# Cross-attention block on one core: the two key halves of the value product moved into the innermost loop

## The chip, the core and the metric

The kernel runs on one core of a Trainium2 chip. The metric is the device time of one execution in microseconds (us). Three executions of the kernel before took 1031.25 us (median), from 1029.74 to 1033.43.

The engines are named as the profile names them: PE is the matrix engine, PEld its loading of weights, DVE the vector engine, ACT the scalar engine, POOL the general engine, SP the engine that issues most transfers. PE writes its results to PSUM, which this kernel uses as eight banks of 512 floats on each of 128 partitions. A matmul of 32 contraction rows and 32 result columns stands in the profile as `32*32`. The kernel places such matmuls by the partitions of the operands (`32c`, the tile's row) and of the result (`32r`, its column); with four of each these are sixteen places, called tiles here.

## The reference

Sixteen batches, 1024 queries and 64 keys each, width 512, 16 heads of 32. Cut to what matters here:

```python
xq  = _ada_ln(x_q,  t_vec, Wss_q,  bss_q)      # layer norm, scale and shift from the condition
xkv = _ada_ln(x_kv, t_vec, Wss_kv, bss_kv)
q   = (xq @ Wq + bq).reshape(B, Lq, nh, dh)
kv  = (xkv @ Wkv + bkv).reshape(B, Lkv, 2, nh, dh)
k, v = kv[:, :, 0], kv[:, :, 1]
scores = jnp.einsum('bqhd,bkhd->bhqk', q, k) / jnp.sqrt(jnp.float32(dh))
attn = jax.nn.softmax(scores, axis=-1)
out  = jnp.einsum('bhqk,bkhd->bqhd', attn, v).reshape(B, Lq, H)
return x_q + (out @ Wp + bp)
```

The change is in the product of `attn` and `v`. Everything is float32.

## The kernel before

The queries are cut into 32 blocks of 512 (`TB`), two to a batch; `i` counts the blocks. The order of all work is written out by hand: after a prologue for the keys, the values and blocks 0 to 2, a loop from line 1404 on runs over blocks 3 to 29, and the last blocks are written out again. In one turn `i` of the loop PE does, in this order and with other products between them: the scores of block `i` (`scores`), the value product of block `i-1` (`mix(a)`), the output projection of blocks `i-2` and `i-1` (`product`), and the query projection of block `i+1` (`query_product`). The two projections use seven products of half blocks in place of eight.

The 64 keys of a batch are two halves of 32, counted by `z`. The scores and the weights of a block lie in two tiles, `s_tiles[i, 0]` and `s_tiles[i, 1]`, one for each half: partitions `32c` to `32c+31` hold the 32 keys of the half for head group `c` (`NC` = 4 groups), and `r` counts the four heads of a group (`HPC` = 4). DVE takes maxima (`maximum`), POOL subtracts them (`subtract`), ACT exponentiates (`weights`), and POOL adds the two halves (`total`) for the row sums, whose inverse comes back through DRAM (`inverse_rows`, `spread_rows`).

`mix(i)` makes the value product. For half `z`, group `c` and head `r` one matmul takes the 32x32 values `vt[rows, z, 32r:32r+32]` as weights and the 32x512 weights of the queries `p[rows, r, :]` as the moving operand, and writes partitions `32r` to `32r+31` of bank `po[c]`. Its array tile is thus row `c`, column `r`: sixteen tiles, each used once for each half, 32 matmuls in all. The second half adds to what the first has written. The loops before are `z` outermost, then `c`, then `r`: a tile is used again after the fifteen others. In 31 of the 32 blocks the four banks are two pairs from the pool that the scores use too (`ps_s`); in block 29 (`apart=False`) they are four single banks.

`divided(i)` on DVE multiplies the finished banks by the inverse row sums and writes `ot`, one pair of banks after the other; `row_sums` on POOL and `product` on PE read `ot`.

The row of the trace for a matmul carries the line of the call: L826 is the matmul of `mix`, L658 that of the scores, L539 that of the query projection (and of the keys' and values'), L955 that of the output projection, L853 and L871 those of its plain form in the first and last blocks. Every float32 matmul that is no transpose is four rows in the trace: a weight load and a product, and then a second weight load and a second product on the same tile.

Of the kernel before, what the change touches and what calls it, by code (L numbers as in the profile page):

```python
# [20 lines left out]
def cross_attention_block(  # L21
# [24 lines left out]
    NC = H // P  # L46
    HPC = P // DH
# [31 lines left out]
    def bank(name, k=None):  # L79
        if k is None:  # L80
            k = ring.pop(0)
            ring.append(k)
        return ps_m.tile([P, TB], F32, tag=f"mm{k}", name=name)
# [563 lines left out]
    s_tiles, m_tiles = {}, {}  # L647
# [162 lines left out]
    def mix(i, apart=True, ks=(None,) * NC):  # L810

        vt = v_tiles[i // BPB]

        if apart:
            pairs = [ps_s.tile([P, 2, TB], F32, tag="s", name=f"po_{i}_{e}") for e in range(2)]
            po = [pairs[c // 2][:, c % 2, :] for c in range(NC)]
            po_tiles[i] = pairs
        else:
            po = [bank(f"po_{i}_{c}", ks[c]) for c in range(NC)]
            po_tiles[i] = po  # L820
        for z in range(2):
            p = s_tiles.pop((i, z))
            for c in range(NC):
                rows = slice(32 * c, 32 * c + 32)
                for r in range(HPC):
                    nc.tensor.matmul(  # L826
                        po[c][32 * r : 32 * r + 32, :],
                        lhsT=vt[rows, z, 32 * r : 32 * r + 32],
                        rhs=p[rows, r, :],
                        start=(z == 0),  # L830
                        stop=(z == 1),
                    )
# [443 lines left out]
    query_out(2, 2)  # L1276
    hidden(4, (0,))
    mix(0)
    subtract(1, zs=(0,))
    spread_rows(0)  # L1280
# [67 lines left out]
    hidden(5, (1,))  # L1348
    query_product(3, 6)
    mix(1)  # L1350
    copied(2, 1, 1)
    copied(2, 1, 0)
# [51 lines left out]
    for i in range(3, NB - 2):  # L1404
# [24 lines left out]
        biased(a, 2)  # L1429
        load_residual(i)  # L1430
        mix(a)
        divided(a)
        row_sums(a, 0)
# [44 lines left out]
    y, z = NB - 2, NB - 1  # L1478
# [134 lines left out]
```

## Time and profile before

| what | before |
|---|---|
| time, median of 3 runs | 1031.25 us (1029.74 to 1033.43) |
| span of the profiled execution | 1029.1 us |
| PE busy | 1009.3 us (98%) |
| weight loads (PEld) busy | 763.4 us (74%) |
| DVE busy | 860.9 us (84%) |
| POOL busy | 805.9 us (78%) |
| ACT busy | 638.6 us (62%) |
| granted TensorE clock, mean | 0.998 |

The profiled execution is one run of the program under the profiler; its span goes from its first to its last instruction, 1029.1 us, and lies 2.1 us under the median of the timed runs. Busy time counts an engine as busy as long as at least one of its rows lasts. The ends of PE's rows are modelled from the size of the instruction, so rows of PE overlap, and what a product costs is read from the starts of successive rows. The chain of waits follows the work back from the last instruction and says at each step what released it. A column `x64` counts rows; a view cut to a stretch of time counts the rows that overlap it. Idle time of an engine that is not the bottleneck costs nothing.

### The profile page before, as it was taken

Reading aid. Unit: us, or ns where it says so; the run is one execution under the profiler, and the core shown is the slowest. Engines: PE = TensorE matmul, PEld = TensorE weight load, DVE = VectorE, ACT = ScalarE, POOL = GpSimd, SP = SyncE. Lnnn points to the kernel's source line nnn. Section 1 sums busy time; section 2 is a strip of 40 time slices with the busy share of each in tenths; the row PEclk is TensorE's granted clock in tenths of the full one; section 3 lists DMA queues with packets and bytes.
Section 4 is the critical chain, followed back from the end, with each engine's and each line's share of the span. In section 5 each row is a group of like instructions: output and inputs, shape, how many; then the busy total and the mean of one; then the engine's idle time right before and its main releaser. Section 6 shows DMA issues by size and latency. Waiting matters only on the chain.

```text
span 1029.1 us, 21212 instructions
## 1 busy us (share of the span) xinstructions
PE 1009.3 (98%) x8077; PEld 763.4 (74%) x8077; DVE 860.9 (84%) x1174; ACT 638.6 (62%) x1025; POOL 805.9 (78%) x518
## 2 busy tenths in 40 slices
PE   8999899999999999999999999999999999999998
PEld 7877556777777777777777778777777777777746
DVE  6686669889888888889898888898888888876795
ACT  3786565666666666667666666666666676665530
POOL 4566687798888888898888888988888888987861
PEclk9999999999999999999999999999999999999999
DMA  9563544444544444445444444445434444335122
GB/s 318 179 188 119 149 122 136 157 157 156 165 155 121 143 128 154 152 152 166 140 134 146 150 133 153 156 159 165 148 110 151 134 154 154 113 125 166 46 85 85
DMA packets 112197, 149.82 MB, mean 146 GB/s; under 512 B 34104, under 2 KB 45392, under 8 KB 112096
## 3 DMA queue, kind: packets, MB, share of 16 engines
q1 hardware_dynamic: 111712, 147.94, 45.3%
q8 instruction: 64, 1.05, 0.4%
q0 software_dynamic: 384, 0.54, 0.3%
q14 instruction: 37, 0.30, 0.1%
HBM read 79.21 MB, written 34.60 MB: 111 GB/s over the span
## 4 chain that ended last, share of the span: by engine, by line
PE 81%; SPq 6%; DMA 5%; DVE 4%; ACT 1%; issue 1%; POOL 1%; DVEq 0%; ACTq 0%; POOLq 0%
PE pp L955 34%; PE pq L539 33%; PE po L826 6%; PE ps L658 6%; SPq L387 4%; DMA ltd<-lt 1%; SPq L631 1%; PE pk_A L539 1%; PE pv_A L539 1%; DMA xt<-ht 1%; DMA r<-in_x_dram 1%; DVE ht L365 1%; DVE lt L762 1%; DMA wss_kv<-in_L_xcond_Wss_kv_dram 1%; DMA x<-in_x_dram 1%
## 5 line engine op out<-in xcount | busy, mean ns | idle before, releaser
L717 POOL TENSOR_TENSOR s<-s,mb 128x2048 f32<-128x2048 f32 x64 | 290.2, 4558 | 129.3 <-DVE mb L704 127.7
L684 ACT COPY s<-ps 128x1024 f32<-128x1024 f32 x128 | 129.4, 1012 | 108.1 <-DVE m L675 64.8
L675 DVE TRANSPOSE_TENSOR_REDUCE m<-ps 128x32 f32<-128x1024 f32 x128 | 150.7, 1213 | 33.6 <-PE ps L658 33.4
L955 PE MATMUL pp<-w_p_sb,ot 128*128 128x256 f32 x720 | 165.6, 379 | 0.5 <-DVE r L979 0.4
L979 DVE TENSOR_TENSOR r<-pp,r 128x512 f32<-128x512 f32 x203 | 131.8, 670 | 30.9 <-PE pp L955 24.3
L578 ACT ACTIVATE qt<-pq,bias_t 128x256 f32<-128x256 f32 x256 | 105.6, 463 | 77.2 <-PE pq L539 77.0
L955 PEld LDWEIGHTS pp<-w_p_sb,ot 128*128 128x128 f32 x720 | 136.6, 190 | 20.5 <-issue 1.6
L723 ACT ACTIVATE s<-s 128x2048 f32<-128x2048 f32 x64 | 122.3, 1911 | 43.8 <-POOL s L717 43.8
L757 POOL TENSOR_TENSOR sum<-s,s 128x2048 f32<-128x2048 f32 x31 | 140.7, 4540 | 7.0 <-ACT s L723 7.0
L955 PEld LDWEIGHTS pp<-WT,s 128*128 128x128 f32 x480 | 86.5, 189 | 57.0 <-issue 37.7
L539 PE MATMUL pq<-xt_sums,w_q_sums 128*128 128x256 f32 x512 | 123.3, 385 | 0.0
L539 PE MATMUL pq<-xt,w_q_sums 128*128 128x256 f32 x512 | 121.1, 379 | 1.6 <-DVE qt L585 1.6
L539 PE MATMUL pq<-xt,w_q_sb 128*128 128x256 f32 x512 | 121.6, 380 | 0.3 <-ACT pq L551 0.2
L539 PEld LDWEIGHTS pq<-xt_sums,w_q_sums 128*128 128x128 f32 x512 | 94.9, 190 | 36.5 <-issue 24.8
L955 PE MATMUL pp<-WT,s 128*128 128x256 f32 x480 | 119.3, 391 | 0.2 <-POOL s L934 0.2
L955 PE MATMUL pp<-WT,ot 128*128 128x256 f32 x480 | 113.6, 379 | 0.6 <-POOL ot L931 0.6
L539 PEld LDWEIGHTS pq<-xt,w_q_sb 128*128 128x128 f32 x512 | 96.8, 190 | 16.4 <-issue 1.7
L539 PEld LDWEIGHTS pq<-xt,w_q_sums 128*128 128x128 f32 x512 | 97.2, 190 | 15.2 <-DVE qt L585 2.0
L955 PEld LDWEIGHTS pp<-WT,ot 128*128 128x128 f32 x480 | 91.0, 190 | 14.1 <-POOL ot L931 1.0
L335 ACT ACTIVATE x<-x,rstdq 128x512 f32<-128x512 f32 x128 | 97.0, 807 | 4.4 <-POOL rstdq L312 4.4
L447 ACT ACTIVATE xt<-xt,ss_q 128x512 f32<-128x512 f32 x124 | 93.9, 808 | 5.1 <-DMA xt<-ht 4.5
L498 POOL TENSOR_TENSOR xt_sums<-xt 128x512 f32<-128x512 f32 x64 | 81.4, 1272 | 14.2 <-ACT xt L447 7.3
(176 smaller groups left out, 1509.8 us busy)
## 6 DMA issues: line engine op xcount, KB each, us to landing
x<-in_x_dram SPq DMA_DIRECT2D x32, 1024.0 KB, 5.5
r<-in_x_dram SPq DMA_DIRECT2D x32, 1024.0 KB, 5.1
xt<-ht SPq DMA_DIRECT2D x488, 64.0 KB, 2.0
out_dram<-r SPq DMA_DIRECT2D x58, 512.0 KB, 3.7
out_dram<-r SPq DMA_DIRECT2D x11, 256.0 KB, 2.2
wss_kv<-in_L_xcond_Wss_kv_dram SPq DMA_DIRECT2D x4, 512.0 KB, 7.3
wss_q<-in_L_xcond_Wss_q_dram SPq DMA_DIRECT2D x4, 512.0 KB, 11.0
vr<-ltd SPq DMA_DIRECT2D x128, 8.0 KB, 1.6
```

Source lines behind the costliest of these rows:

```text
L335: nc.scalar.activation(dst, src, AF.Identity, bias=rstd[:, 1, j : j + 1], scale=rstd[:, 0, j : j + 1])
L447: nc.scalar.activation(xt[:, :, c, :], xt[:, :, c, :], AF.Identity, scale=ss["q"][:, c, b : b + 1], bias=ss["q"][:, NC + c, b : b + 1],)
L498: eng.tensor_tensor(dst, a, b, ALU.subtract)
L539: nc.tensor.matmul(out_, lhsT=lhsT, rhs=rhs, start=new and m == 0 and c == 0, stop=c == HC - 1, skip_group_check=True,)
L578: nc.scalar.activation(dst, src, AF.Identity, bias=bq_t[:, o : o + 1])
L675: nc.vector.tensor_reduce(m_tiles[i][:, z, 2 * e : 2 * e + 2, :], s_banks[i, z][e].rearrange("p r (j a) -> p r j a", a=32), AX.X, ALU.max, ...
L684: nc.scalar.copy(s_tiles[i, z][:, 2 * e : 2 * e + 2, :], s_banks[i, z][e])
L717: eng.tensor_tensor(s_tiles[i, z], s_tiles[i, z], mb_tiles[i], ALU.subtract)
L723: nc.scalar.activation(p, p, AF.Exp, scale=SCALE)
L757: nc.gpsimd.tensor_tensor(t, s_tiles[i, 0], s_tiles[i, 1], ALU.add)
L955: nc.tensor.matmul(acc[k][:, t * HO : (t + 1) * HO], lhsT=rows[:, c, t * P : (t + 1) * P], rhs=cols[:, c, :], start=n == 2 and t == 0 and ...
L979: nc.vector.tensor_add(r, a, r)
```

## The change

In `mix`, both tiles of weights are taken out of `s_tiles` ahead of the loops, and the loop over the halves becomes the innermost one:

```diff
-        for z in range(2):
-            p = s_tiles.pop((i, z))
-            for c in range(NC):
-                rows = slice(32 * c, 32 * c + 32)
-                for r in range(HPC):
+        p = [s_tiles.pop((i, z)) for z in range(2)]
+        for c in range(NC):
+            rows = slice(32 * c, 32 * c + 32)
+            for r in range(HPC):
+                for z in range(2):
                     nc.tensor.matmul(
                         po[c][32 * r : 32 * r + 32, :],
                         lhsT=vt[rows, z, 32 * r : 32 * r + 32],
-                        rhs=p[rows, r, :],
+                        rhs=p[z][rows, r, :],
                         start=(z == 0),
                         stop=(z == 1),
                     )
```

The 32 matmuls of a block, their operands, their tiles and their banks are the same. Their order on PE is now tile by tile, the two halves of a tile directly behind each other. No other instruction of any engine is added, removed or moved against the others.

## The prediction, on record before the changed kernel had run

> **What bounds the kernel now.** I read the page first, then the chain of waits, then windows from one value product to the next.
>
> ```profile
> PE 1009.3 (98%) x8077; PEld 763.4 (74%) x8077; DVE 860.9 (84%) x1174; ACT 638.6 (62%) x1025; POOL 805.9 (78%) x518
> PE 81%; SPq 6%; DMA 5%; DVE 4%; ACT 1%; issue 1%; POOL 1%; DVEq 0%; ACTq 0%; POOLq 0%
> ...
> 206.64:235.83 29.19, 29.19 (x242) 22.31 (x241) 25.88 (x35) 19.16 (x30) 24.41 (x16) 1.00 0.48 150
> 907.27:936.46 29.19, 29.19 (x242) 22.31 (x241) 22.74 (x27) 15.49 (x21) 23.63 (x12) 1.00 0.36 112
> ```
>
> The last two rows are stretches from the start of one value product to the next (length, then PE, PEld, DVE, ACT, POOL busy, granted clock). PE is busy for all of 29.19 us, the next engine for 25.88. There are (936.46 - 206.64) / 29.19 = 25 such turns, so 26 value products stand where each nanosecond that PE loses is lost by the kernel. The other six stand ahead of 206.64 (three) or behind 936.46 (three), where others wait too.
>
> So the question is how long PE needs for 32 matmuls on sixteen tiles in the new order. One value product in the middle of the run, matmuls and weight loads, in rows of ever narrower windows:
>
> ```profile
> L826 PE MATMUL po<-s,V_A x1024: 584/588/612, 107.0 to 558.7; 32*32 32x512 f32 x171
> ...
> 527.76 0.23 PEld L826 LDWEIGHTS po<-s,V_A 32*32 32x32 f32 x32 [0.33 <-ACT x L335]
> 528.22 0.10 PEld L826 LDWEIGHTS po<-s,V_A 32*32 32x32 f32 x1 [0.22 <-issue]
> 528.65 0.10 PEld L826 LDWEIGHTS po<-s,V_A 32*32 32x32 f32 x1 [0.33 <-issue]
> 528.84 0.12 PEld L826 LDWEIGHTS po<-s,V_A 32*32 32x32 f32 x2
> 528.65 0.55 PEld L826 LDWEIGHTS po<-s,V_A 32*32 32x32 f32 x31 [0.33 <-issue]
> 529.53 0.59 PE L826 MATMUL po<-s,V_A 32*32 32x512 f32 x1
> 530.04 0.48 PE L539 MATMUL pq<-xt_sums,w_q_sums 128*128 128x256 f32 x1
> ...
> 527.87:528.21 0.34, 0.34 (x16) 0.13 (x31) 1.00 0.27 66
> 528.23:528.33 0.10, 0.10 (x32) 0.10 (x1) 1.00 0.37 82
> 528.66:528.83 0.17, 0.17 (x17) 0.10 (x1) 1.00 0.05 12
> ```
>
> The 1024 rows on V_A belong to 16 blocks of 32 matmuls, so a matmul is two products (a pass each) and two weight loads. What the rows show, from the start at 527.77:
>
> - All 32 loads of the first half are issued within 0.23 us, and until 528.21 exactly sixteen products are in flight: the first pass of every tile. The program's order is first and second pass of tile 0, then tile 1; so products of different tiles do overtake each other, and a tile does its own in order.
> - Tile 0's passes follow its weight loads' release: second pass at 528.22 (0.45 us after the first), first pass of the other key half at 528.65 (0.43 later). Four passes of one tile in a row thus start over 0.45 + 0.43 + 0.43 = 1.31 us.
> - Between 528.66 and 528.83 there are 17 products: 16 old ones and tile 0's third. Tiles 1 to 15, free from 528.66 on, get nothing: the next load comes at 528.84. Something holds back the 35th load.
> - From there the remaining 30 loads (31 rows from 528.65, without that one) are spread up to 529.20 less 0.10 for the last, 529.10: 0.26 us for 15 tiles, 0.017 us for the four instructions of a matmul. In the first half they came at 0.10 / 15 = 0.007 (32 loads in 0.23, of which 0.10 is the last one's length and 0.03 its lag behind the first).
> - The product of another shape starts 0.51 us behind the last start (529.53 to 530.04). Total: 2.28 us.
>
> What holds the 35th load? Sixteen matmuls are 64 instructions, and the loads fit a **queue of 64** places that come free in program order, each when its instruction is over by its modelled end. Load 33, a product and load 34 are instructions 65 to 67 and get the places of tile 0's first three; instruction 68 needs the place of the fourth, tile 0's second pass, which ends at 528.22 + 0.588 = 528.81, and load 35 is right behind it: 0.03 us later. The first value product of the run, which had only eight products under way where the other has sixteen, tells this from a drain of the whole array:
>
> ```profile
> 107.06:107.09 0.03, 0.03 (x8) 0.03 (x17) 1.00 0.24 68
> 527.85:527.88 0.03, 0.03 (x16) 0.03 (x29) 1.00 1.89 410
> ...
> 107.43 0.10 PEld L826 LDWEIGHTS po<-s,V_A 32*32 32x32 f32 x1
> ...
> 108.05 0.10 PEld L826 LDWEIGHTS po<-s,V_A 32*32 32x32 f32 x1
> ```
>
> These are its 33rd load (at tile 0's second pass) and its 35th: 107.43 + 0.588 + 0.03 = 108.05, the same distance, although its later tiles were late. The Trainium skill says in "TensorE: Matmul & The Clock Gate", section "Architectural detail: the array is 16× 32×32, not 1× 128×128", that TensorE's queue is 64 deep and a partial reorder window; the trace agrees with its 64 places.
>
> **The change part by part.** It removes and adds no instruction; it reorders 32 matmuls in each of 32 blocks (2 x 1024 rows, 64 to a block). Now a tile has eight instructions one behind the other, so 64 places hold eight tiles, not sixteen. Step by step, from the start of a block:
>
> 1. Tiles 0 to 7 enter at 2 x 0.007 us from each other and do their four passes side by side: starts at 0, 0.45, 0.88, 1.31, the last pass over at 1.31 + 0.59 = 1.90.
> 2. Tile 8's instructions take the places of tile 0's as these end: its first pass at 0.61 + 0.03 = 0.64, its last at 1.93.
> 3. Tile 9 needs the places of tile 1, which come free only behind all of tile 0's: 1.90 + 0.03 = 1.93. Tiles 9 to 15 then enter at 2 x 0.017 us from each other; tile 15 starts at about 2.14.
> 4. Tile 15's last pass starts at 2.14 + 1.31 = 3.45, and the next product 0.51 behind it: 3.96 us.
>
> So a block needs 3.96 us for 2.28, **1.68 us more**; the pause of 0.19 us at 528.65 and the slower entry are gone, and a wait of half the tiles for the other half has come.
>
> Does anything cover it? Within a turn no: PE has no idle time. What is queued behind on PE all moves with it. On DVE, `divided` takes the first pair of banks about when it did (tile 7's last pass is over at 1.99; before, the pair was taken at 2.3), the second pair at about 4.1 (3.45 + 0.59):
>
> ```profile
> 530.08 2.36 DVE L806 TENSOR_TENSOR ot<-po,vb 128x1024 f32<-128x1024 f32 x2 [0.43 <-issue]
> 532.04 3.45 PE pp L955 x16
> ```
>
> With half of 2.36 us for a pair it is done at 5.3, 1.3 us behind the end of the value product on PE; `product` with the first pair starts 1.92 behind that (530.12 to 532.04) and with the second 1.73 later, so no new wait. DVE's 25.88 us of work have room in 30.87.
>
> The six at the ends. PE waits there for others, and the lost time goes into those waits:
>
> ```profile
> PE pp L871 <- ACT pp L866: 2.9, 1, 2.9
> PE pq L539 <- DVE qt L585: 1.6, 1, 1.6
> PE pq L539 <- ACT qt L578: 1.3, 1, 1.3
> ...
> 116.36 10.26 DMA r<-in_x_dram
> 152.75 2.06 DMA xt<-ht
> 181.02 0.39 DMA xt<-ht
> ...
> 188.40 3.69 PE pq L539 x16
> ```
>
> The chain of waits runs through the residual's load at 116.36 and the moves at 152.75 and 181.02, not through PE; PE takes it over at 188.40. Block 0's 1.68 goes into the wait of 2.9, block 1's into the 1.6, block 2's into the 1.3, with 0.35 left over. At the end:
>
> ```profile
> 979.75 0.70 PE L853 MATMUL pp<-w_p_sb,ot 128*128 128x512 f32 x1 [0.68 <-DVE ot L801]
> 983.01 1.19 DVE L675 TRANSPOSE_TENSOR_REDUCE m<-ps 128x32 f32<-128x1024 f32 x1
> ...
> 992.53 3.70 PE L853 MATMUL pp<-w_p_sb,ot 128*128 128x512 f32 x8
> 997.35 0.65 DVE L882 TENSOR_TENSOR r<-pp,r 128x512 f32<-128x512 f32 x1
> ...
> 1010.31 1.99 PE L955 MATMUL pp<-WT,ot 128*128 128x256 f32 x8
> 1012.44 3.72 PE L955 MATMUL pp<-w_p_sb,ot 128*128 128x256 f32 x16
> 1016.36 1.59 PEld L955 LDWEIGHTS pp<-WT,s 128*128 128x128 f32 x8 [0.60 <-POOL s L934]
> ```
>
> Block 29: the scores behind it are wanted by DVE only at 983.01, so nothing. Block 30: L853 ends at 996.23 + 1.68 = 997.91, and DVE, which took it at 997.35, takes it at about 997.95: 0.6. Block 31: the eight rows at 1010.31 go to 1011.99, 1.73 for them and 3.45 for the sixteen (3.45 for sixteen rows at 532.04) bring PE to 1017.18, where it waited until 1016.36: 0.8.
>
> Sum: 26 x 1.68 = 43.7, and 0.35 + 0.6 + 0.8: **45.4 us**. The profiled execution goes from 1029.1 to 1074.5; the median of the runs lies 2.15 above that span, so 1031.25 + 45.4 = **1076.6 us**.
>
> The bounds. The trace shows no tile with more than four instructions waiting or under way, so what PE does with eight on one tile is not shown. From below: were no place short, a block would be 1.31 + 15 x 0.013 + 0.51 = 2.02 us, 0.26 less than now. From above: were tile 1 held until tile 0 has taken its fourth load (0.88), 15 x 0.88 + 1.31 + 0.51 = 15.0 us, 12.8 more. I take the queue of 64, since it gives the 2.28 and the pause of the old order from the same rows.
>
> **The rivals.**
>
> *A tile takes only its next weights, and the queue stops there.* Tile 0's instructions for the other half wait for its first half, and tile 1's stand behind them: 12.8 us a block. 32 x 12.8 = 410, less the 2.9 + 1.6 + 1.3 of waits ahead and 3 x 1.68 - 1.4 = 3.6 behind: about 1430 us. For it: weights 33 and 34 came only when tile 0 took them (528.22, 528.65). Against it: tiles did pass a waiting pass of tile 0, and the 35th load waited for 528.81, not 528.65. 0.11. A stricter form: products start in the program's order. A tile would have to start its fourth pass before the next starts its first: 16 x 1.31 + 0.51 = 21.5 us, 19.2 more a block, some 1640 us. Sixteen first passes under way before any second speak against it. 0.01. (The Trainium skill has this as a rule, "TensorE: Matmul & The Clock Gate", section "The mechanism": matmuls start and end in strict order. The trace disagrees.)
>
> *Faster: the pause was the price of coming back to a tile late, not of a full queue.* Then tile 8 finds place at once, and each of 26 blocks, and part of the six, gains 0.26: 7 to 8 us, 1024 us. It decides if tile 9's first pass starts within 0.2 us of tile 0's. For it: the pause stands just where tiles are used again. Against it: it ended with tile 0's pass, in both blocks. 0.05.
>
> *No change that can be measured.* Between the two, with something like 0.1 us a block. 0.03. That the order is not what the change says can be left out: PE's order is written by hand.
>
> **How the numbers follow.** 0.80 for the forecast, 0.11, 0.01, 0.05, 0.03. This kernel's measurement can tell 0.3% from no change (3 us). Slower 0.92, same 0.03, faster 0.05. Within the forecast: all 32 blocks paid in full give 32 x 1.68 = 53.8, 1085 us; a tile's entry at 0.017 for all and a queue a few places off move a block by 0.2, some 6 us either way. 1062 to 1092 holds the forecast's case, and with it 8 in 10.
>
> **What would show it.** In the changed kernel a stretch between value products of 30.87 us with PE busy throughout; in the value product sixteen weight loads of eight tiles in the first 0.2 us, one tile more at 0.6, seven from 1.93 on; the last start near 3.45. It is wrong if tile 9 starts before 1.8 us or tile 1 after 0.1, or if PE shows new waits for DVE L806.

## The result: 4.4% slower, and the profile after

The changed kernel takes 1077.11 us (median of 4 runs, 1076.26 to 1078.6) against 1031.62 us for the kernel before (4 runs): a ratio of 1.044, 95% interval 1.0423 to 1.0457. The prediction was 1076.6 us. The profiled execution spans 1076.8 us, 47.7 more than before; the other three runs span 1074.5 to 1075.4.

The page of the changed kernel, engines first, then the chain of waits by engine and by line:

```profile
PE 1061.0 (99%) x8077; PEld 798.0 (74%) x8077; DVE 866.6 (80%) x1174; ACT 641.4 (60%) x1025; POOL 805.3 (75%) x518
PE 89%; DMA 4%; SPq 3%; DVE 2%; ACT 1%; POOL 1%; issue 1%; DVEq 0%; POOLq 0%
PE pp L955 34%; PE pq L539 33%; PE po L826 11%; PE ps L658 6%; SPq L387 2%; PE pp L853 1%; PE pk_A L539 1%; PE pv_A L539 1%; DMA r<-in_x_dram 1%; DMA xt<-ht 1%; DMA ltd<-lt 1%; DMA wss_kv<-in_L_xcond_Wss_kv_dram 1%; POOL sum L757 0%; POOL s L717 0%; DVE ht L365 0%
```

The counts are those of before, PE's busy time is up by 51.7 us, and the value product (L826) has gone from 6% of the chain to 11%. The other engines do the same work in a longer span, so their shares fall.

Stretches from the start of one value product to the next, changed kernel:

```profile
207.84:238.71 30.87, 30.87 (x241) 23.35 (x240) 26.08 (x35) 19.27 (x30) 24.36 (x16) 1.00 0.47 140
948.70:979.57 30.87, 30.87 (x241) 23.35 (x240) 22.97 (x27) 15.60 (x21) 23.61 (x12) 1.00 0.36 108
```

A turn is 30.87 us for 29.19, PE busy for all of it, at a granted clock of 1.00: 1.68 us a turn.

One value product of the changed kernel (it starts at 609.14), weight loads of the whole block, then single loads, the last product and the first of another shape, then how many products and loads are in flight in four stretches:

```profile
609.14 0.23 PEld L826 LDWEIGHTS po<-s,V_B 32*32 32x32 f32 x17 [0.33 <-ACT x L335]
609.60 0.72 PEld L826 LDWEIGHTS po<-s,V_B 32*32 32x32 f32 x18 [0.23 <-issue]
610.64 0.10 PEld L826 LDWEIGHTS po<-s,V_B 32*32 32x32 f32 x1 [0.33 <-issue]
611.07 1.19 PEld L826 LDWEIGHTS po<-s,V_B 32*32 32x32 f32 x28 [0.33 <-issue]
612.59 0.59 PE L826 MATMUL po<-s,V_B 32*32 32x512 f32 x1
613.11 0.48 PE L539 MATMUL pq<-xt_sums,w_q_sums 128*128 128x256 f32 x1
...
609.25:609.59 0.34, 0.34 (x8) 0.12 (x16) 1.00 0.11 30
609.70:609.78 0.08, 0.08 (x16) 0.08 (x8) 1.00 0.85 230
611.00:611.07 0.07, 0.07 (x9) 0.00 (x0) 1.00 0.70 176
611.30:611.50 0.20, 0.20 (x8) 0.11 (x7) 1.00 0.01 0
```

Read it against the block of before. There, 32 loads went out at once and sixteen tiles worked; here it is 17 loads (two for each of tiles 0 to 7, and tile 8's first), and until 609.59 exactly eight products are in flight: tiles 0 to 7. They take their second passes from 609.60 on; the sixteen products at 609.70 are the first and second passes of these same eight tiles, because the first ones are still in flight by their modelled ends. Tile 8 takes tile 0's places one by one, the fourth load at 610.64. Tile 9 gets its first load at 611.07, when tile 0's last pass is over (609.14 + 1.90 = 611.04), and the 28 loads of tiles 9 to 15 follow from there. At 611.00 nine products are in flight, at 611.30 eight: the array is half empty for most of the block. The last product starts 3.45 us after the first, and the next shape 0.52 later, 3.96 us in all.

### The profile page after: what moved, and what is told of

Its sections match the earlier page's. It is cut to its first block, busy times and chain, and to the rows that moved or that the text cites. A ratio compares the mean times of both kernels' runs of the same rounds, so it can differ in the third digit from the quotient of the medians.

```text
span 1076.8 us, 21212 instructions
## 1 busy us (share of the span) xinstructions
PE 1061.0 (99%) x8077; PEld 798.0 (74%) x8077; DVE 866.6 (80%) x1174; ACT 641.4 (60%) x1025; POOL 805.3 (75%) x518
## 4 chain that ended last, share of the span: by engine, by line
PE 89%; DMA 4%; SPq 3%; DVE 2%; ACT 1%; POOL 1%; issue 1%; DVEq 0%; POOLq 0%
PE pp L955 34%; PE pq L539 33%; PE po L826 11%; PE ps L658 6%; SPq L387 2%; PE pp L853 1%; PE pk_A L539 1%; PE pv_A L539 1%; DMA r<-in_x_dram 1%; DMA xt<-ht 1%; DMA ltd<-lt 1%; DMA wss_kv<-in_L_xcond_Wss_kv_dram 1%; POOL sum L757 0%; POOL s L717 0%; DVE ht L365 0%
## 5 line engine op out<-in xcount | busy, mean ns | idle before, releaser
L675 DVE TRANSPOSE_TENSOR_REDUCE m<-ps 128x32 f32<-128x1024 f32 x128 | 154.4, 1237 | 39.9 <-PE ps L658 39.7
L806 DVE TENSOR_TENSOR ot<-po,vb 128x1024 f32<-128x1024 f32 x62 | 75.6, 1224 | 28.5 <-PE po L826 18.7
```

What stands on the lines that cost most here:

```text
L675: nc.vector.tensor_reduce(m_tiles[i][:, z, 2 * e : 2 * e + 2, :], s_banks[i, z][e].rearrange("p r (j a) -> p r j a", a=32), AX.X, ALU.max, ...
```

## The experiments

**1. Eight tiles at a time.** From the changed kernel: the loops of `mix` put in another order, with the halves inside each pair of banks. The loops are written as one list; the call in them is the same and two steps less indented, and is left out below.

```diff
-        for c in range(NC):
+        for c, r, z in [(c, r, z) for e in range(2) for z in range(2) for c in (2 * e, 2 * e + 1) for r in range(HPC)]:
             rows = slice(32 * c, 32 * c + 32)
-            for r in range(HPC):
-                for z in range(2):
...
```

By this edit the call of `mix` stands on line 824, in runs 1 to 4; in run 5 it stands on line 829, and the output projection on 953 and 958.

> The value product goes over eight tiles at a time: the first key half of banks 0 and 1, their second half, then the same for banks 2 and 3. Queue of 64 places freed in program order: tile 0's four instructions end at 1.04 us, not 1.90, so tile 8 enters then; worked through with the distances of the trace of before a block takes 3.00 us (2.28 before, 3.96 in the changed kernel), the last pass starts at 2.49, and the run comes to about 1031.6 + 26 x 0.72 + 1 = 1051 us. Rival, at most eight tiles open at a time, or the two pairs of banks one after the other: the first eight tiles do their two halves before the others begin, as in the changed kernel: 3.9 to 4.0 us a block, 1077 us.

Measured: 1050.13 us, ratio 1.0183 (1.0158 to 1.0208). A turn and its value product in the chain of waits, and the loads of that block:

```profile
593.91:623.82 29.91, 29.91 (x241) 22.70 (x241) 25.98 (x35) 19.29 (x30) 24.40 (x16) 1.00 0.44 142
...
593.98 3.00 PE po L824 x64
...
593.91 0.23 PEld L824 LDWEIGHTS po<-s,V_B 32*32 32x32 f32 x17 [0.33 <-ACT x L335]
594.37 0.85 PEld L824 LDWEIGHTS po<-s,V_B 32*32 32x32 f32 x32 [0.23 <-issue]
595.41 0.10 PEld L824 LDWEIGHTS po<-s,V_B 32*32 32x32 f32 x1 [0.20 <-issue]
595.84 0.23 PEld L824 LDWEIGHTS po<-s,V_B 32*32 32x32 f32 x14 [0.33 <-issue]
```

3.00 us a block, 29.91 a turn: 0.72 more than before, as the queue gives it. In this order, too, 64 instructions hold eight tiles, but tile 0's four first ones are over 0.86 us earlier, so the second eight enter in the middle of the block (32 loads from 594.37 to 595.22). The rival would have kept them out to the end of the first eight, 3.9 to 4.0 us; it falls.

**2. Heads first.** From the changed kernel: the two outer loops exchanged, so that the first eight tiles lie on all four banks (again as one list, without the call).

```diff
-        for c in range(NC):
+        for c, r, z in [(c, r, z) for r in range(HPC) for c in range(NC) for z in range(2)]:
             rows = slice(32 * c, 32 * c + 32)
-            for r in range(HPC):
-                for z in range(2):
...
```

> The key halves stay innermost, but the heads are the outer loop and the four banks the inner one, so the first eight tiles lie on all four banks and all four rows of the array. Queue of 64 places: which tile it is does not matter, 3.96 us a block with the same starts as in the changed kernel, 1077 us; DVE gets both pairs of banks only at the end (4.1 us), and its first product still comes 0.5 us before PE wants it. Rival, the second pair of banks or rows 2 and 3 have to wait for the first: nothing is left to wait for, 2.0 to 2.3 us a block, about 1030 us.

Measured: 1079.26 us, ratio 1.0458 (1.0436 to 1.0481).

```profile
609.76:640.63 30.87, 30.87 (x241) 23.35 (x240) 25.99 (x35) 19.29 (x30) 24.40 (x16) 1.00 0.43 139
...
609.83 3.96 PE po L824 x64
```

The turn and the block are those of the changed kernel to 0.01 us. Which row, column or bank the late tiles lie on does not matter, and so the second pair of banks is not what tiles 8 to 15 wait for. DVE gets both pairs only at the end of the block, and PE's turn is no longer for it. The run is 2 us longer than the changed kernel's, with intervals that overlap; in its profile the first value product starts at 109.85, 1.4 us later than in the changed kernel's (108.42), and up to there both do the same work.

**3 and 4. One pass to a matmul.** Both kernels take the upper halves of the floats as bfloat16, which leaves the lower 16 bits of each operand of the value product out; a matmul is then one load and one product, 64 instructions a block in place of 128. Run 3 has the halves outermost, run 4 innermost. Both are edits of the changed kernel, with the loops written as one list; the operands change like this:

```diff
-                        lhsT=vt[rows, z, 32 * r : 32 * r + 32],
-                        rhs=p[z][rows, r, :],
+                        lhsT=vt[rows, z, 32 * r : 32 * r + 32].bitcast(mybir.dt.bfloat16)[:, 1::2],
+                        rhs=p[z][rows, r, :].bitcast(mybir.dt.bfloat16)[:, 1::2],
```

> The value product takes the upper halves of its floats as bfloat16 operands, so a matmul is one weight load and one product, with the key halves outermost as before. All 64 instructions of a block have a place in a queue of 64. Both theories: sixteen tiles at once, two passes each; with a pass between 0.21 and 0.43 us (not shown by the trace for this type) 0.9 to 1.4 us a block. This is the measure for the next run.

> The same upper halves as bfloat16 operands, with the key halves innermost as in the changed kernel. Queue of 64 places: 32 loads and 32 products all find a place, no tile waits for a place, and the block takes what it takes with the halves outermost, within 0.1 us; the runs are the same within 0.3%. Rival, at most eight tiles open at a time (or a cost of the order in itself): the second eight begin when the first have ended, two passes of 0.21 to 0.43 us later, 0.4 to 0.9 us a block, 12 to 27 us a run.

Measured: 1021.62 us with the halves outermost (ratio 0.9902, 0.9882 to 0.9923), 1021.50 us with the halves innermost (0.9909, 0.9883 to 0.9935). The run times alone would not be enough, because PE is no longer busy all the time in these two: a stretch of run 3 shows 28.00 us of PE in 28.80, and the chain runs through POOL and ACT.

```profile
580.61:609.41 28.80, 28.00 (x212) 21.53 (x211) 25.80 (x35) 19.17 (x30) 24.40 (x16) 1.00 0.48 153
...
579.27 9.08 POOL s L717 x2
588.35 0.02 issue
588.37 1.91 ACT s L723
590.29 0.74 ACT qt L578 x2
```

So the block itself has to be read. Run 3 first, then run 4, loads, products and the next shape:

```profile
580.61 0.19 PEld L824 LDWEIGHTS <-V_B 32*32 32x32 bf16 x32 [0.33 <-issue]
580.61 0.67 PE L824 MATMUL po<-s,V_B 32*32 32x512 bf16 x32
581.22 0.48 PE L539 MATMUL pq<-xt_sums,w_q_sums 128*128 128x256 f32 x1
```

```profile
579.93 0.20 PEld L824 LDWEIGHTS <-V_B 32*32 32x32 bf16 x32 [0.33 <-issue]
579.93 0.72 PE L824 MATMUL po<-s,V_B 32*32 32x512 bf16 x32
580.58 0.48 PE L539 MATMUL pq<-xt_sums,w_q_sums 128*128 128x256 f32 x1
```

In both all 32 loads go out within 0.2 us. The block takes 0.61 us with the halves outermost and 0.65 with them innermost: the order costs 0.04 us where it cost 1.68. The rival needed 0.4 to 0.9 and falls. The expected 0.9 to 1.4 us was too high, but not because of the pass: in both traces tile 0's second product starts 0.24 us behind its first, inside the 0.21 to 0.43 allowed. The range comes out as two passes and 0.51 us to the next shape. The rows show only one pass between the first starts and the last ones: the last product of run 3 ends at 581.28 and takes 0.38 us, so it starts at 580.90, 0.29 us behind the first. The next shape comes 0.32 us behind that start, where float32 needed 0.51.

**5. The halves apart.** If a block's second half loses time because the first still fills the queue, the kernel before should gain by parting them. From the kernel before: `mix` split by halves, in the loop from line 1404.

```diff
+        mix(a, zs=(0,))
         product(b, 3)
         spread_rows(a)
...
         load_residual(i)
-        mix(a)
+        mix(a, zs=(1,))
         divided(a)
```

> From the kernel before: in the loop over blocks 3 to 29 the first key half of the value product goes ahead of the projection product that stood in front of it, the second stays where it was; the 128x128 product lies between them. Each half is 64 instructions, so neither waits for a place. Queue of 64 places: each half takes what sixteen such matmuls of the scores take, 1.07 us from its first product to the next one, 2.14 for 2.28, and 27 turns of 0.14 are 3.7 us: 1027.9 us, a turn of 29.05. Rival, coming back to a tile costs the pause in itself, or two more changes of shape cost what is won: no change, 29.19 us a turn.

Measured: 1031.77 us (12 runs) against 1030.94 us (17 runs), ratio 1.0009, 0.9997 to 1.0021: no gain. A turn, and the chain of waits through both halves:

```profile
525.46:554.71 29.25, 29.25 (x242) 21.90 (x241) 26.07 (x35) 19.17 (x31) 24.39 (x15) 1.00 0.47 148
...
523.81 1.73 PE pq L539 x8
525.53 1.07 PE po L829 x32
526.60 1.93 PE pp L958 x8
528.53 1.07 PE po L829 x32
529.60 1.93 PE pq L539 x8
```

Each half takes 1.07 us, as expected, 2.14 for 2.28. But eight rows of a product that stands behind a block of the other shape take 1.93 us, and 1.73 where no change of shape is ahead of it. The split adds one such change: 0.20 for 0.14 won, 29.25 for 29.19. The rival's second arm decided; the mechanism of the halves was right, and the expectation had left the change of shape out of the sum.

## Why the prediction was right, point by point

**PE is the bound, and each turn pays in full.** Right: 30.87 us a turn with PE busy throughout, and 25 turns between 207.84 and 979.57 take 41.9 us more than those from 206.64 to 936.46.

**A queue of 64 places, freed in program order, each when its instruction is over by its modelled end.** Right as far as the runs go. It gave 3.96 us for the block and 3.96 was measured; with the same numbers it gave 3.00 for eight tiles at a time (3.00), 3.96 for heads first (3.96), and no cost of the order where the whole block fits (0.04). The 1.07 us of a half alone (1.07 measured) had been read from the rows of the scores; the queue says only that nothing holds such a half back.

The run times do not tell whether places count instructions or products: loads and products stand one to one in all runs, so 64 instructions and 32 products are nearly the same limit. One row points to instructions. The prediction had sixteen loads in the first 0.2 us, and there are seventeen; the last of them, tile 8's first, starts at 609.27, when no product was over yet. That is 0.03 us behind the end of tile 0's first load (609.14 + 0.10), the distance that the other places show. At the pace of tiles 0 to 7 (2 x 0.007 us each) it would have come at 609.25 if loads took no places. Run 1 has the same: its first load starts at 593.91, its seventeenth at 594.04. A difference of 0.02 us is thin, and no run with another proportion of loads and products was tried.

**The pause of 0.19 us and the slower entry are gone, a wait of half the tiles has come.** Right for the pause and the wait: eight products in flight until 609.59, nine at 611.00, eight at 611.30. The slower entry is not gone, and the prediction's own third step has it: tiles 9 to 15 come in from 611.07 to 611.28 (the last start, 612.59, less the 1.31 of four passes), about 2 x 0.017 us a tile.

**No new wait on DVE, and none of PE's for `divided`.** Right for PE in the 25 turns from 207.84 to 979.57, where it waits for nobody. Ahead of them there is one new wait for DVE L806, 0.2 us at 150.59; by its letter the prediction's last sentence counts it as a sign of being wrong, but it touches none of the 26 blocks. DVE now does wait in the middle of `divided`, as expected from the second pair's late end, and the turn is no longer for it:

```profile
DVE ot L806 <- PE po L826: 18.7, 29, 1.0
```

**The two rivals that hold a tile back** (a tile takes only its next weights, or strict program order, 1430 and 1640 us) are out: seventeen loads within 0.23 us and eight tiles with first passes side by side. **Faster** is out with the same rows: tile 9 starts 1.93 us behind tile 0.

A slip in the prediction's sums changes nothing: 15.0 us a block for 2.28 is 12.7 more, not 12.8.

**The ends** came out otherwise. Expected were 0.35 us ahead of the 25 even turns and 1.4 behind them, besides block 28's own 1.68; in the profiled executions it is 1.2 (207.84 for 206.64) and 47.7 - 41.9 - 1.2 - 1.7 = 2.9.

The 1.2 ahead cannot be put down to the change. The first value product, up to which all the kernels do the same work, already starts 1.4 us later (108.42 for 106.98), and over the seven profiles of this case it starts anywhere from 105.84 to 109.85. Run 1, whose blocks cost 0.72 us more than those of the kernel before, has its even turns begin at 205.08, earlier than that kernel's 206.64. So the profiles scatter here by more than the forecast 0.35. But the waits that were to swallow the lost time did not shrink as forecast: the one for DVE L585, meant for block 1, is still there, while the one for ACT L866 shrank by 2.2:

```profile
PE pq L539 <- DVE qt L585: 1.6, 1, 1.6
...
PE pp L871 <- ACT pp L866: 0.7, 1, 0.7
```

Why the prologue's waits moved as they did was not followed up.

The tail was mis-sized. I had put block 29 down as free, because DVE wants its scores late. The chain of the changed kernel shows what I overlooked, PE's own work behind it:

```profile
1025.25 10.50 PE pp L853 x24
1035.74 3.96 PE po L826 x64
1039.71 3.63 PE pp L853 x8
1043.34 3.47 PE pp L955 x16
```

In the kernel before, the chain ran through DVE, POOL and ACT here, and PE waited; now it stays on PE up to 1046.81. Of the 2.9 us, 0.6 were lost at block 29 (forecast: nothing), 1.5 at block 30 (forecast: 0.6) and 0.8 at block 31, as forecast.

**How near the number came is in part luck.** 1076.6 was forecast and 1077.11 measured, but the tail was 1.5 us too small, the four runs go from 1076.26 to 1078.6, and the start of the first value product alone moves by 4 us between profiles. The spans of the three runs that were not profiled (1074.5 to 1075.4, against 1074.5 forecast) say that the profiled execution was the longest of the four. What is no luck is the 1.68 us in each of 26 blocks, which the traces show one by one.

## What to carry to other kernels

Where small matmuls share the array, count instructions in program order: with four to a float32 matmul, the distance between two uses of a tile decides how many tiles 64 places can hold, and sixteen tiles need the sixteen matmuls of the next half to stand behind the sixteen of this one, as before. Derive such a limit from the starts inside one block of the kernel before (which load comes late, and what ended just then): here the starts inside one block gave the block's time in three other orders to 0.01 us. When work on the bound engine grows, look for its own next work at the ends of the program, not only for who waits for its result.

## What the runs showed of the hardware that I had not expected

- Going from the full array to 32x32 tiles and back costs about 0.20 us each time (1.93 us for the eight full-array products behind the tiles, for 1.73 without), more than the 0.14 us that a better order inside the block could win.
- With the value product cut from 2.28 to 0.61 us (run 3), a turn shrinks only from 29.19 to 28.80: 0.39 of the 1.67 us is won. In the stretch shown PE stands idle for 0.80; the remaining 0.5 was not followed up. The chain now runs through maxima on DVE, subtraction on POOL (9.08 us for both halves), the weights on ACT (1.91), and behind them on ACT the query copies that PE waits for. PE's 29.19 us a turn before and this chain's 28.80 lie 1.3% apart.
